# Attention and three binary convolutions on one core: the weighted sums copied out of PSUM by two engines, and the 3x3's products moved ahead in the TensorE order

## The chip, the cores and the metric

The kernel runs on one core of one Trainium2 chip. The metric is the device time of one execution in microseconds (us), lower is better.

## The reference

Two layers act on x of shape (8, 64, 64, 64), eight images of 64 channels and 4096 pixels. The first is an attention over the pixels of each image with an extra "unary" term, the second the sum of a 1x1, a 3x3 and a 5x5 convolution of signs with signs, scaled by a gate per channel. Cut to what matters:

```python
q, k, v = wq@x + bq, wk@x + bk, wv@x + bv          # 64 x 4096 per image
q, k = q - q.mean(pixels), k - k.mean(pixels)
out = softmax(q^T k / 8) applied to v               # 4096 x 4096 per image
out = out + v @ softmax(q_mean . k)                 # the unary term
x = x + out
# second layer
s = sum over k in (1, 3, 5) of bn_k(conv_k(sign(x + move_k), sf_k * sign(w_k - mean)))
gate = sigmoid(grouped 16x16 linear of mean(s))
return s * gate + x
```

## The kernel before

Two images make a **pair**: 128 partitions are two times 64 channels. There are four pairs, done one after the other. A pair's 4096 queries are cut into eight **blocks** of 512 (`QB`), so there are 32 blocks, numbered g = 0 to 31 in `attend`.

Within a block, `for j in range(NK)` goes over 32 groups of 128 keys. Each step issues the scores of step j (`scores`, L474: matmuls into a two-bank PSUM tile `ps` of the pool `ps_s`, which has two such tiles), then exp on ScalarE (L485), then the weighted sums of step j-1 (`weighted`, L493: matmuls that add into `acc`), and on VectorE the sum of the exponentials (`summed`, L506 and L508). So when j = 0 of block g runs, the last weighted sums of block g-1 are still to come; after them the block's own extra work is issued, in an order written out by hand in `plan`: `put(i, f)` issues f after step i.

[...]`ps_s` has two tiles of two banks, `ps_a` one tile of two banks (tag `acc`), `ps_m` two tiles of one bank (tag `m`). The two banks of `acc` hold, per query block, the weighted sums of the two halves of each key group. A tile of a pool takes over the banks of an older one, and waits until that one has been read.

At step 0 of block g the order is:

1. `weighted_out` of block g-1 (L515): ScalarE copies the two banks of `acc` to SBUF, as one tile `o` of 128 x 1024.
2. `send` and `gather` (L522, L530): SP's queue takes the sums of the exponentials through DRAM to spread them over partitions.
3. `mix_rows`: TensorE makes the queries of block g+1 (`split_queries`, L460, into two `m` tiles `pq`, read out by VectorE at L467 and by ScalarE at L468), and from g = 3 on the convolutions of block g-3. At the end of the mix come the read-outs.
4. In some blocks small extra matmuls: `unary_end` (g = 1, 8, 16, 24), `mean_scores` (g = 4, 12, 20), `mean_rows_out` (g = 2).

In `mix_rows` two sequences run side by side on the two row halves of TensorE's array, the rows h = 0 and h = 1, for both images at once, so one step is four small matmuls. Each product has a length in units (0.5 for a product of the 3x3 or 5x5, 1.0 for the 1x1, 2.0 for the queries), and the steps are sorted by it. The second sequence holds products of the 5x5, named A, B and D (25). The first holds the 10 products S of the 5x5, the 1x1, and the 12 of the 3x3, named A, B, S and D too, three of each. The 5x5's S, A and B are in a two-bank tile of `ps_s`, its D and the 1x1 in `m` tiles; the latter take over the banks of the two `pq`, the 1x1 that of L467. **The 3x3 is in a two-bank tile of `ps_a`, the banks of `acc`.** It therefore comes between the weighted sums of block g-1 and those of block g.

The results leave PSUM by `begin_rows` (ScalarE, L729: the 1x1), `hold_rows` (ScalarE, L734: the 3x3, after its last product) and `add_rows` (VectorE, L744 twice and L750: the 5x5's A, B and S). At step 12 of the block, `added` (VectorE, L582) adds the two halves of `o`, and `finish` (L586, L587) divides and adds the residual.

In the last block `weighted_out` is called after the loop with two parts of 320 and 192 columns, since the rest of the work hangs on it. The first queries of all are made in a two-bank tile of `ps_s` and read by VectorE (L442) and ScalarE (L443); the second ones, read by the same two lines, in two `m` tiles. A fallback at the end, for inputs whose exponentials leave the range, does not run here.

The semaphores between engines are set by the tile framework that the kernel is written in. The order of the instructions on each engine is that of the source (`tc.manual_schedule()`).

Of the kernel before, what the change touches and what calls it, by code (L numbers as in the profile page):

```python
# [22 lines left out]
ALU = mybir.AluOpType  # L23
# [3 lines left out]
P = 128  # L27
# [4 lines left out]
QB = 512  # L32
# [12 lines left out]
def conv_seq_kernel(ctx, tc, x, wq, wk, wv, vecs, w1, w3, w5, wtap, gw, out):  # L45
    nc = tc.nc
# [9 lines left out]
    fp = ctx.enter_context(tc.tile_pool(name="fp", bufs=1))  # L56
# [6 lines left out]
    def m_tile(name):  # L63
        return ps_m.tile([P, QB], F32, tag="m", name=name)
# [180 lines left out]
    def n_products(k, name):  # L245
        return k if k == 3 or name == "D" else 2 * k
# [10 lines left out]
    class Pair:  # L257
# [252 lines left out]
        def weighted_out(self, qb, parts=(slice(0, QB),)):  # L510

            acc = self.acc[qb]
            self.acc[qb] = self.tile(fp, "o", qb, (P, 2, QB))
            for c in parts:
                nc.scalar.copy(self.acc[qb][:, :, c], acc[:, :, c])  # L515

# [59 lines left out]
        def added(self, qb, cols=slice(0, QB)):  # L578
            if cols.start == 0:
                self.x2[qb] = self.tile(bp, "x2", qb)  # L580
            acc = self.acc[qb]
            nc.vector.tensor_tensor(self.x2[qb][:, cols], acc[:, 0, cols], acc[:, 1, cols], ALU.add)  # L582

        def finish(self, qb, cols=slice(0, QB)):
            x2 = self.x2[qb][:, cols]
# [295 lines left out]
    def mix_rows(q, c):  # L881


        seqs = [[], []]
        if q is not None:
            for h in range(2):
                seqs[h].append((("q",), 0, 2.0))
        if c is not None:
            p, (r0, _, y) = c
            qb = r0 // ROWS  # L890

            def products(k, name):
                return [((k, name), i, 0.5) for i in range(n_products(k, name))]

            S = products(5, "S")
            three = [t for name in "ABSD" for t in products(3, name)]
            seqs[0] += S[:8] + [((1,), 0, 1.0)] + three + S[8:]
            seqs[1] += products(5, "A") + products(5, "B") + products(5, "D")
        order = []
        for h, seq in enumerate(seqs):  # L900
            at = 0.0
            for t in seq:
                order += [(at, h, b, t) for b in (h, 1 - h)]
                at += t[2]
        order.sort(key=lambda o: o[0:2])
        if q is not None:
            q[0].query_tiles(q[1])
        z, left = {}, {}
        for o in order:
            left[o[3][0]] = left.get(o[3][0], 0) + 1  # L910
        half = [slice(0, QB // 2), slice(QB // 2, QB)]
        for _, h, b, (n, i, _) in order:
            if n == ("q",):
                q[0].split_queries(q[1], b, h)
            else:
                if n not in z:
                    name = f"{p.name}_{qb}_{n[0]}"
                    if n == (1,):
                        z[n] = m_tile(f"z{name}")
                    elif n == (5, "D"):  # L920
                        z[n] = m_tile(f"z{name}d")[:, half[0]]
                    elif n[0] == 3:
                        z3 = ps_a.tile([P, 2, QB], F32, tag="acc", name=f"z{name}")
                        for j, m in enumerate("ABSD"):
                            z[3, m] = z3[:, j // 2, half[j % 2]]
                    else:
                        t = score_banks(f"z{name}")
                        z[5, "S"], z[5, "A"], z[5, "B"] = t[0][:, half[0]], t[1][:, half[0]], t[1][:, half[1]]
                if n == (1,):
                    p.conv_tap((r0, ROWS, y), [[z[n]]], b, 0, 0, 0, True, True)  # L930
                else:
                    p.row_product(z[n], b, *n, i, r0)
            left[n] -= 1
            if left[n] == 0 and n == ("q",):
                q[0].split_queries_out(q[1])
            elif left[n] == 0 and n == (1,):
                p.begin_rows(qb, z[n])
            elif left[n] == 0 and n == (3, "D"):
                p.hold_rows(qb, z3)
        if c is not None:  # L940
            p.add_rows(qb, z[5, "A"], z[5, "B"], z[5, "S"])
            p.z5d = z[5, "D"]
# [21 lines left out]
    def attend(pairs):  # L964
# [9 lines left out]
        def plan(g):  # L974
# [17 lines left out]
            def both():  # L992
                q = block(g + 1) if g + 1 < n_blocks else None
                if g == 0:
                    mix(q, None)
                else:
                    mix_rows(q, rows(g - 3) if g >= 3 else None)
# [291 lines left out]
```

## Time and profile before

| | |
|---|---|
| median of 3 runs | 1933.31 us (1933.23 to 1934.18) |
| profiled execution | 1934.02 us, of which the span from the first to the last instruction is 1931.8 us |
| granted TensorE clock | 0.998 |
| TensorE busy | 1914.2 us, 99% of the span |
| VectorE busy | 1594.1 us, 83% |
| ScalarE busy | 1274.0 us, 66% |
| scores, L474 | 8192 matmuls, 590 ns each |
| weighted sums, L493 | 8192 matmuls, 590 ns each |
| L485 exp, ScalarE | 1024 of 1025 ns |
| L508 sums of exp, VectorE | 960 of 1220 ns |
| L515 copy of `acc`, ScalarE | 31 of 128x1024 at 1006 ns, and two shorter at the end |
| L467 and L468 queries out | 30 of 484 ns and 30 of 490 ns |
| L734 `hold_rows` | 29 of 1114 ns |

Matmuls overlap, so the ends of single ones are modelled and the busy share of TensorE says that it is hardly ever without work, not that it runs at its peak. What matters is the distance between the starts of successive groups: eight matmuls, 0.86 us, for one step's scores or weighted sums. "PEld" is TensorE's weight load. An engine's idle time is put down to what ended it.

### The profile page before, as it was taken

How to read it: one execution, taken by the hardware profiler on the slowest of the kernel's cores; microseconds unless marked ns; L12 is line 12 of the kernel's file. 1: busy time of each engine (PE TensorE's matmuls, PEld its weight loads, DVE VectorE, ACT ScalarE, POOL GpSimd, SP SyncE). 2: the span in 40 equal slices, each digit the busy share in tenths (PEclk: the TensorE clock that was granted, in tenths of full speed). 3: DMA queues.
4: the chain of work that ended last, by engine and by line, in shares of the span. 5: the costliest groups of instructions: out<-in, count | busy, mean ns of one | idle time of the engine just before them, and what ended most of it. 6: DMA issues, size and time to landing. Idle time of an engine off the chain costs nothing.

```text
span 1931.8 us, 48355 instructions
## 1 busy us (share of the span) xinstructions
PE 1914.2 (99%) x20848; PEld 754.9 (39%) x20848; DVE 1594.1 (83%) x2066; ACT 1274.0 (66%) x1523; POOL 5.9 (0%) x26
## 2 busy tenths in 40 slices
PE   9999999999999999999999999999999999999997
PEld 4333343343333333343433333433443333333334
DVE  6878888889887888888888888898887888877876
ACT  5667766666666766666666676666666666666663
POOL 0000000000000000000000000000000000000000
PEclk9999999999999999999999999999999999999999
DMA  3021110110112110101101211011011011111111
GB/s 101 31 70 29 28 40 32 40 35 16 40 35 80 56 51 27 41 32 40 35 16 40 84 53 57 28 29 40 32 40 35 16 56 50 49 39 37 25 35 46
DMA packets 58998, 80.58 MB, mean 42 GB/s; under 512 B 15628, under 2 KB 40600, under 8 KB 58648
## 3 DMA queue, kind: packets, MB, share of 16 engines
q1 hardware_dynamic: 58024, 76.22, 12.9%
q8 instruction: 165, 2.70, 0.6%
q10 hardware_dynamic: 720, 1.18, 0.2%
q14 instruction: 57, 0.47, 0.1%
q0 software_dynamic: 32, 0.01, 0.0%
HBM read 39.27 MB, written 24.77 MB: 33 GB/s over the span
## 4 chain that ended last, share of the span: by engine, by line
PE 97%; DVE 1%; ACT 1%; DMA 0%; issue 0%; SPq 0%; DVEq 0%
PE ps L474 46%; PE acc L493 45%; PE z L703 4%; PE pv L313 1%; PE pq L460 1%; PE z L785 1%; ACT e L485 0%; DMA x<-in_x 0%; DVE es L508 0%; PE warm L155 0%; DVE r L576 0%; PE z_5d L703 0%; DMA out<-sb 0%; ACT o L515 0%; ACT rc_ck L418 0%
## 5 line engine op out<-in xcount | busy, mean ns | idle before, releaser
L485 ACT ACTIVATE e<-ps 128x1024 f32<-128x1024 f32 x1024 | 1049.7, 1025 | 597.8 <-PE ps L474 576.8
L508 DVE TENSOR_TENSOR es<-es,e 128x1024 f32<-128x1024 f32 x960 | 1171.2, 1220 | 187.6 <-ACT e L485 158.2
L474 PE MATMUL ps<-q,x 64*64 64x512 f32 x8192 | 1069.5, 590 | 0.9 <-DVE kb L165 0.9
L493 PE MATMUL acc<-e,v 64*64 64x512 f32 x8192 | 1065.2, 590 | 0.6 <-ACT e L485 0.3
L493 PEld LDWEIGHTS acc<-e,v 64*64 64x64 f32 x8192 | 307.6, 131 | 577.8 <-ACT e L485 305.9
L474 PEld LDWEIGHTS ps<-q,x 64*64 64x64 f32 x8192 | 312.2, 133 | 528.9 <-issue 278.0
L703 PE MATMUL z<-e,wt 64*64 64x256 bf16 x754 | 69.3, 270 | 0.1
L703 PE MATMUL z<-ec,wt 64*64 64x256 bf16 x754 | 69.4, 270 | 0.0
L744 DVE SCALAR_TENSOR_TENSOR sb<-z,scale,sb 128x256 f32<-128x256 f32 x29 | 14.0, 483 | 65.4 <-PE z L703 62.2
L703 PEld LDWEIGHTS <-wt 64*64 64x64 bf16 x1508 | 65.0, 105 | 0.4 <-issue 0.4
L703 PE MATMUL z<-ec,wc 64*64 64x256 bf16 x464 | 60.5, 270 | 0.0
L506 DVE TENSOR_TENSOR es<-e,e 128x1024 f32<-128x1024 f32 x32 | 39.2, 1225 | 24.5 <-ACT e L485 24.5
L703 PEld LDWEIGHTS <-wc 64*64 64x64 bf16 x1218 | 55.6, 106 | 4.8 <-issue 0.6
L619 ACT ACTIVATE s<-x,vec 128x512 bf16<-128x512 f32 (+2 forms) x66 | 46.1, 702 | 5.2 <-DVE x L587 5.2
L757 DVE TENSOR_TENSOR sb<-sb,es_z 128x256 f32<-128x256 f32 x116 | 43.9, 420 | 1.0
L703 PE MATMUL z<-e,wc 64*64 64x256 bf16 x319 | 44.4, 270 | 0.0
L734 ACT ACTIVATE es_z<-z,frac 128x1024 f32<-128x1024 f32 x29 | 32.3, 1114 | 16.3 <-PE z L703 16.3
L515 ACT COPY o<-acc 128x1024 f32<-128x1024 f32 (+2 forms) x33 | 32.3, 981 | 1.2 <-PE acc L493 1.2
L467 DVE TENSOR_SCALAR q<-pq,mx 128x256 f32<-128x256 f32 x30 | 14.5, 484 | 20.8 <-PE pq L460 20.8
L313 PEld LDWEIGHTS pv<-wx,x 64*64 64x64 f32 x1024 | 21.6, 134 | 17.8 <-issue 9.2
L703 PE MATMUL z<-s,wc 64*64 64x256 bf16 x145 | 25.4, 270 | 0.0
L587 DVE SCALAR_TENSOR_TENSOR x<-x,ou,x 128x512 f32<-128x512 f32 (+2 forms) x33 | 24.3, 735 | 1.2
(156 smaller groups left out, 743.6 us busy)
## 6 DMA issues: line engine op xcount, KB each, us to landing
es<-es SPq DMA_DIRECT2D x31, 512.0 KB
e_parts<-es SPq DMA_DIRECT2D x124, 128.0 KB
r<-rc SPq DMA_DIRECT2D x62, 128.0 KB
x<-in_x SPq DMA_DIRECT2D x15, 512.0 KB
out<-sb SPq DMA_DIRECT2D x28, 256.0 KB
ec<-e SPq DMA_DIRECT2D x29, 153.0 KB
xc<-in_x SPq DMA_DIRECT2D x60, 64.0 KB
ec<-e SPq DMA_DIRECT2D x29, 132.0 KB
```

The lines of the kernel that those rows point to most:

```text
L313: nc.tensor.matmul(pv[img[h], b, i * w : (i + 1) * w], self.x[img[b], bass.ds((4 * g + i) * P + h * H, H)], self.wx[img[b], :], start=True ...
L474: nc.tensor.matmul(ps[img[h], b, :], self.x[img[b], bass.ds(j * P + h * H, H)], self.q[qb][img[b], :], start=True, stop=neg is None,)
L485: nc.scalar.activation(e, ps, AF.Exp, scale=1.0 / 8.0)
L493: nc.tensor.matmul(self.acc[qb][img[b], h, :], self.v[img[h], j, img[b]], e[img[h], b, :], start=(j == 0), stop=(j == NK - 1),)
L506: nc.vector.tensor_tensor(self.es[qb], self.first, e, ALU.add)
L508: nc.vector.tensor_tensor(self.es[qb], self.es[qb], e, ALU.add)
L515: nc.scalar.copy(self.acc[qb][:, :, c], acc[:, :, c])
L587: nc.vector.scalar_tensor_tensor(x2, x2, self.ou, self.x[:, bass.ts(qb, QB)][:, cols], ALU.add, ALU.add)
L619: nc.scalar.activation(sy[n][0][:, rows, pad : pad + HH], self.x2[qb][:, r0 * HH : r1 * HH].rearrange("p (h w) -> p h w", w=HH), AF.Sign, ...
L703: nc.tensor.matmul(z[img[b], :].rearrange("p (h w) -> p h w", w=HH), taps[img[h], c * C : c * C + C], src[:, first : first + 3 * step + 1 ...
L734: nc.scalar.activation(z, two, AF.Identity, scale=frac[3][:, 0:1])
L757: nc.vector.tensor_tensor(out, out, self.z3[i], ALU.subtract if (i, t) == (3, 1) else ALU.add)
```

## The change

Three edits. `weighted_out` copies the two banks of `acc` with two instructions in place of one: ScalarE copies the first bank to a tile `o0`, VectorE the second to a tile `o1`. `added` adds the two tiles. In `mix_rows`, the first sequence was eight products S, the 1x1, the twelve of the 3x3, two S; it becomes five S, six of the 3x3 (A and B), the 1x1, six of the 3x3 (S and D), five S. The number of matmuls is the same.

```diff
         def weighted_out(self, qb, parts=(slice(0, QB),)):

             acc = self.acc[qb]
-            self.acc[qb] = self.tile(fp, "o", qb, (P, 2, QB))
+            self.acc[qb] = [self.tile(fp, f"o{h}", qb) for h in range(2)]
             for c in parts:
-                nc.scalar.copy(self.acc[qb][:, :, c], acc[:, :, c])
+                nc.scalar.copy(self.acc[qb][0][:, c], acc[:, 0, c])
+                nc.vector.tensor_copy(self.acc[qb][1][:, c], acc[:, 1, c])
...
             acc = self.acc[qb]
-            nc.vector.tensor_tensor(self.x2[qb][:, cols], acc[:, 0, cols], acc[:, 1, cols], ALU.add)
+            nc.vector.tensor_tensor(self.x2[qb][:, cols], acc[0][:, cols], acc[1][:, cols], ALU.add)
...
             S = products(5, "S")
             three = [t for name in "ABSD" for t in products(3, name)]
-            seqs[0] += S[:8] + [((1,), 0, 1.0)] + three + S[8:]
+            seqs[0] += S[:5] + three[:6] + [((1,), 0, 1.0)] + three[6:] + S[5:]
             seqs[1] += products(5, "A") + products(5, "B") + products(5, "D")
```

## The prediction

> **What bounds the kernel now.** I read the page's engine table first, then the waits, then the timeline of one block boundary, because the change touches nothing else.
>
> ```profile
> PE 1914.2 (99%) x20848; PEld 754.9 (39%) x20848; DVE 1594.1 (83%) x2066; ACT 1274.0 (66%) x1523; POOL 5.9 (0%) x26
> ACT e L485 <- PE ps L474: 576.8, 865, 3.1
> DVE sb L744 <- PE z L703: 62.2, 28, 2.2
> PEld acc L493 <- ACT es_z L734: 22.2, 29, 0.9
> DVE q L467 <- PE pq L460: 20.8, 29, 0.7
> ```
>
> The first line is the engine table, the others are from the waits (who waited for whom: us in total, times, longest). TensorE is the bound: ScalarE and VectorE wait for it, not it for them. What it loses near this change, it loses where a block of 512 queries ends, 31 times. There, 29 times, its weight load waits for ScalarE's L734 (`hold_rows`), and 29 times VectorE stands idle 0.72 us (20.8/29) before it copies the queries out.
>
> The timeline at the boundary near 602 us (start, us, engine, line, out<-in, idle before):
>
> ```profile
> 601.61 1.04 PE L493 MATMUL acc<-e,v 64*64 64x512 f32 x8
> 602.77 1.01 ACT L515 COPY o<-acc 128x1024 f32<-128x1024 f32 x1
> 603.13 0.48 DVE L467 TENSOR_SCALAR q<-pq,mx 128x256 f32<-128x256 f32 x1 [0.72 <-PE pq L460]
> 603.78 0.38 PE L785 MATMUL z<-y,wt 64*64 64x512 bf16 x2
> 605.54 1.11 ACT L734 ACTIVATE es_z<-z,frac 128x1024 f32<-128x1024 f32 x1 [0.56 <-PE z L703]
> 605.68 1.03 PE L474 MATMUL ps<-q,x 64*64 64x512 f32 x6
> 606.71 1.09 PE L493 MATMUL acc<-e,v 64*64 64x512 f32 x8
> 607.62 0.61 PE L474 MATMUL ps<-q,x 64*64 64x512 f32 x4
> ```
>
> Query products start at 602.46, the products of the convolutions at 602.89, one step of four small matmuls every 0.11 us, 25 steps. The 1x1 starts at step 8, the 3x3 at step 10 (604.00). The 3x3 uses the `acc` banks, so it must follow the copy L515, which ends at 603.78: 0.2 us to spare, no wait. At the other end `hold_rows` ends at 606.65 and only then do the next weighted sums start, at 606.71. The scores before them (605.68) take 0.86 us in the steady loop, so 606.54 was possible; with the exposed weight load the next scores start at 607.62 instead of 607.41. **The bubble is 0.205 us.** Start times at all 28 boundaries from 189 to 1781 us show it 22 times; in the other six (near 250, 488, 722, 961, 1194, 1433 us), where `unary_end` or `mean_scores` puts extra matmuls before the scores, there is none. The most that can be gained is thus about 22 x 0.205 = 4.5 us, 0.23%.
>
> [...] VectorE COPY out of PSUM takes 290 ns for 128 columns and 356 for 192, 1.03 ns a column. [...]
>
> **Do the two copies run side by side?** The kernel leaves semaphores to its tile framework, so I looked for two engines that read one two-bank PSUM tile. There is one place: the first queries, whose `pq` is a tile of the scores pool, bank 0 read by VectorE (L442), bank 1 by ScalarE (L443). A second time the same two lines read two separate tiles. The timeline of the two engines there:
>
> ```profile
> 12.18 0.74 DVE L442 TENSOR_SCALAR q<-pq,mx 64x512 f32<-64x512 f32 x1
> 13.02 0.68 ACT L443 ACTIVATE q<-pq,nmx 64x512 f32<-64x512 f32 x1 [1.91 <-DVE kb L165]
> 14.89 1.02 ACT L485 ACTIVATE e<-ps 128x1024 f32<-128x1024 f32 x1 [1.19 <-PE ps L474]
> 15.94 0.68 ACT L443 ACTIVATE q<-pq,nmx 64x512 f32<-64x512 f32 x1
> L443 ACTq EVENT_SEMAPHORE  x1: 17/17/17, 12.9 to 12.9; - x1
> ```
>
> The first L443 was idle 1.91 us. Its data were ready (`pq` before 7.7 us, `nmx` at 12.20), yet its EVENT_SEMAPHORE (last line, from the answer for that source line) passed only at 12.9 and it started at 13.02; L442 had ended at 12.92. The second L443 has no such semaphore, though it too writes `q` beside L442. What differs is the shared PSUM tile. L744 points the same way: it reads products A in one bank, all done by 605.3, and starts at 605.84, after the last S product in the other bank. So waits go by tile, not bank, reads against reads included. `acc` is such a tile. **I take it that the VectorE copy waits for the ScalarE copy**, and that the 3x3, which takes over the tile, waits for both.
>
> **The change, part by part** (boundary near 602 us).
>
> 1. ScalarE copies 512 columns instead of 1024: 586 ns (L321, the same shape from PSUM) instead of 1006, 602.77 to 603.36. ScalarE is not the bound; its saved 0.42 us is covered by TensorE.
> 2. VectorE copies 512: no row has it. From the slope, 290 + 384 x 1.03 = 686 ns (upper end 743, L442's time). It starts 0.03 us after ScalarE's: 603.39 to 604.08. Queued behind it is L467: 604.0 to 604.5, 0.87 us late. Who waits: the 1x1 takes L467's bank, but comes later (604.80), so nothing; the new `q` is wanted a block later.
> 3. The 3x3 moves from step 10 to step 5, 603.45 undisturbed. It now needs the VectorE copy: 604.08 + 0.04 to pass the semaphore + about 0.03 of exposed weight load = 604.15. **Stall 0.70 us** (0.62 if the wait hides behind a loaded weight and the copy is short, 0.80 with the longest copy). [...] everything behind stalls: 1x1, S, A, B, D, the scores. No DMA moves: SP issues its `send` and `gather` as before, ahead of these products.
> 4. The 3x3 ends three steps earlier relative to the rest, so `hold_rows` starts 0.33 us earlier in relative terms. Its own predecessor on ScalarE, the 1x1's L729, comes 0.33 us later and just clears. Then it ends about 0.2 us before the weighted sums want the banks: the bubble of 0.205 goes. What is late next is the release of the S, A, B banks (L750 ends 607.17 + 0.70), which the second scores meet with a few hundredths to spare.
> 5. L582 adds two SBUF tiles instead of halves of one: same 684 ns.
>
> Sum: 22 boundaries x (0.70 - 0.205) = 10.9. Six without a bubble x 0.70 = 4.2. The one at 1840 us (no query products, copy already late by 0.26): 3x3 released at 1841.07, 20 steps follow, scores 0.88 later less the bubble: 0.7. The first two have no convolutions, but `unary_end` (76.45) and `mean_rows_out` (133.18) use L467's bank and wait for it already: L467 later by 0.65 and 0.86: 1.5. Last block: two parts, each copied by both engines, alternating (0.43, 0.49, 0.32, 0.36 us by the slopes): L582 moves from 1905.39 to 1906.25, the reciprocals L576 from 1905.89 to 1906.66: 0.8. **Total +18.1 us.** The profiled execution took 1934.02 (span 1931.8), 0.71 above the median of 1933.31; on the median the forecast is 1951.4.
>
> **Rivals.** A measurement of this kernel can tell about 0.2%, 3.9 us, from no change.
> - *Side by side, wait by tile.* VectorE starts when TensorE's last sum is done, 602.70 to 603.39, inside its 0.72 us of idle time. The 3x3's weights can load at 603.43: stall at most 0.05. Gain 22 x 0.16 - 6 x 0.05 = 3.2, less 0.8 for L467 in the first two blocks: 1930.9. [...] Against: the semaphore at 12.9 us. It decides if the VectorE copy starts before ScalarE's ends; with its extras it wins while the stall is under 0.13 us, that is with the copy over by about 603.5.
> - *One after the other, but each half of the 3x3 waits for its own bank.* A and B need ScalarE's half (603.41), S and D come at 604.32, after VectorE's. No stall: gain 4.5, less 1.5 and 0.8: 1931.1. Against: L744.
> - *Side by side without any stall* and little lost in the first two blocks: 22 x 0.205 = 4.5, 1929 or a little less, just past what can be told. That needs waits by bank throughout.
>
> **How the numbers follow.** One after the other 0.85 (slower); side by side by tile or each half by its bank 0.10 (the same); no stall at all 0.05 (faster). Within the first, the stall of 0.62 to 0.80 gives 15.8 to 20.9; without first blocks and tail 2.3 less, with unseen waits of 0.1 at each boundary about 3 more: 1946 to 1957, and I reach one lower.
>
> **What would show it.** Right: a VectorE COPY `o1` starting 0.03 us after ScalarE's `o0` ends, 686 ns long; TensorE's first 3x3 product waiting 0.6 to 0.8 us for it, 29 times, some 20 us in all; the wait of L493 for L734 gone; L467 near 1.6 us after the queries begin. Wrong: both copies starting within 0.1 us of each other, or no wait of L703 for VectorE.

## The result

The changed kernel takes **1949.58 us** (median of 4, 1948.93 to 1950.35) against 1933.74 for the kernel before in the same comparison (1933.23 to 1934.77): the ratio is 1.0081, 95% interval 1.0064 to 1.0099. It is 15.8 us slower; 18.1 were forecast, and the measured time lies within the forecast range. The profiled execution has a span of 1947.1 us, 15.3 more than before, at the same granted clock of 0.998.

The page of the changed kernel, its span, its engines and two of its groups:

```profile
span 1947.1 us, 48392 instructions
PE 1915.5 (98%) x20848; PEld 895.2 (46%) x20848; DVE 1612.2 (83%) x2099; ACT 1257.2 (65%) x1523; POOL 5.9 (0%) x26
L704 PE MATMUL z<-e,wt 64*64 64x256 bf16 x754 | 74.8, 271 | 14.9 <-DVE o L516 14.9
L516 DVE COPY o<-acc 128x512 f32<-128x512 f32 (+2 forms) x33 | 22.3, 676 | 29.8 <-ACT o L515 29.8
```

VectorE has 18 us more to do and ScalarE 17 less, as the edit says, and neither matters. What matters stands at the end of the last two lines (idle time before the group, and what ended how much of it): the VectorE copy is held 29.8 us by the ScalarE copy, and TensorE's products by the VectorE copy. The waits of the changed kernel:

```profile
DVE o L516 <- ACT o L515: 29.8, 32, 1.0
PE z L704 <- DVE o L516: 14.9, 29, 0.9
PEld acc L493 <- ACT es_z L735: 13.6, 26, 0.6
```

And its timeline at the same boundary as before (line numbers after L515 are one higher):

```profile
606.32 0.58 ACT L515 COPY o<-acc 128x512 f32<-128x512 f32 x1
606.78 0.49 ACT L468 ACTIVATE q<-pq,nmx 128x256 f32<-128x256 f32 x1
606.93 0.69 DVE L516 COPY o<-acc 128x512 f32<-128x512 f32 x1 [0.97 <-ACT o L515]
607.54 0.48 DVE L467 TENSOR_SCALAR q<-pq,mx 128x256 f32<-128x256 f32 x1
607.67 0.27 PE L704 MATMUL z<-e,wt 64*64 64x256 bf16 x1 [0.50 <-DVE o L516]
609.47 1.10 ACT L735 ACTIVATE es_z<-z,frac 128x1024 f32<-128x1024 f32 x1
609.78 0.61 PE L474 MATMUL ps<-q,x 64*64 64x512 f32 x2
610.64 1.17 PE L493 MATMUL acc<-e,v 64*64 64x512 f32 x8
```

The copies are not side by side. ScalarE's ends at 606.90, VectorE's begins at 606.93 and ends at 607.62, TensorE's first 3x3 product follows at 607.67. VectorE's read-out of the new queries (L467) now comes 0.76 us after ScalarE's (L468), which does not wait for the second copy. The last two lines are the first scores after the mix and the weighted sums behind them.

### The profile page after: what moved, and what is told of

Read it like the earlier page. It is cut to its first block, busy times and chain, and to the rows that moved or that the text cites. A ratio compares the mean times of both kernels' runs of the same rounds, so it can differ in the third digit from the quotient of the medians.

```text
span 1947.1 us, 48392 instructions
## 1 busy us (share of the span) xinstructions
PE 1915.5 (98%) x20848; PEld 895.2 (46%) x20848; DVE 1612.2 (83%) x2099; ACT 1257.2 (65%) x1523; POOL 5.9 (0%) x26
## 4 chain that ended last, share of the span: by engine, by line
PE 94%; ACT 3%; DVE 2%; issue 0%; DMA 0%; DVEq 0%
PE ps L474 45%; PE acc L493 43%; PE z L704 3%; ACT e L485 2%; DVE o L516 1%; ACT o L515 1%; PE pv L313 1%; PE z L786 1%; PE warm L155 0%; DVE es L508 0%; DVE r L577 0%; PE z_5d L704 0%; DMA out<-sb 0%; ACT rc_ck L418 0%; PE po L363 0%
## 5 line engine op out<-in xcount | busy, mean ns | idle before, releaser
L474 PE MATMUL ps<-q,x 64*64 64x512 f32 x8192 | 1115.1, 590 | 0.9 <-DVE kb L165 0.9
L493 PE MATMUL acc<-e,v 64*64 64x512 f32 x8192 | 1112.4, 589 | 0.6 <-ACT e L485 0.3
L474 PEld LDWEIGHTS ps<-q,x 64*64 64x64 f32 x8192 | 398.6, 133 | 442.9 <-issue 223.4
L493 PEld LDWEIGHTS acc<-e,v 64*64 64x64 f32 x8192 | 355.2, 131 | 525.0 <-ACT e L485 307.8
L704 PE MATMUL z<-e,wt 64*64 64x256 bf16 x754 | 74.8, 271 | 14.9 <-DVE o L516 14.9
L704 PE MATMUL z<-ec,wt 64*64 64x256 bf16 x754 | 74.7, 272 | 0.0
L730 ACT ACTIVATE sb<-z,shift,scale 128x512 f32<-128x512 f32 x29 | 22.6, 778 | 44.4 <-PE z L786 44.4
L516 DVE COPY o<-acc 128x512 f32<-128x512 f32 (+2 forms) x33 | 22.3, 676 | 29.8 <-ACT o L515 29.8
L321 ACT COPY v<-pv 128x512 f32<-128x512 f32 x32 | 18.8, 586 | 9.3 <-PE pv L313 9.2
```

Of the source, the lines that this page charges most:

```text
L474: nc.tensor.matmul(ps[img[h], b, :], self.x[img[b], bass.ds(j * P + h * H, H)], self.q[qb][img[b], :], start=True, stop=neg is None,)
L493: nc.tensor.matmul(self.acc[qb][img[b], h, :], self.v[img[h], j, img[b]], e[img[h], b, :], start=(j == 0), stop=(j == NK - 1),)
L516: nc.vector.tensor_copy(self.acc[qb][1][:, c], acc[:, 1, c])
L704: nc.tensor.matmul(z[img[b], :].rearrange("p (h w) -> p h w", w=HH), taps[img[h], c * C : c * C + C], src[:, first : first + 3 * step + 1 ...
```

## The experiments

**Theory:** the framework's semaphores keep order by PSUM tile. Two engines that only read different banks of one tile wait for each other, and whoever takes the tile over waits for both. **Rivals:** the moved order itself costs the time; or two engines cannot read PSUM at once, whatever the semaphores say; or the second engine is what matters, not the tile.

Diffs are against the changed kernel, except in "Which part of the two-tile kernel does it", where they are against the two-tile kernel with both engines; they show what matters. The kernels were timed against the kernel before (1933.78 us; for the change itself, 1933.74). "Regular" is the mean delay per block over the 22 boundaries that had a bubble, "other six" over those without one, taken from the starts of the scores and weighted sums in the two traces (a block here runs from the last weighted sums of one block to the last of the next).

| kernel | median, us | ratio (95%) | regular, us | other six, us |
|---|---|---|---|---|
| the change | 1949.58 | 1.0081 (1.0064 to 1.0099) | +0.45 | +0.74 |
| new order only | 1940.10 | 1.0032 (1.0019 to 1.0044) | +0.16 | +0.44 |
| two copies only | 1938.96 | 1.0027 (1.0018 to 1.0037) | +0.15 | +0.14 |
| VectorE's copy first | 1949.47 | 1.0078 (1.0065 to 1.0092) | +0.40 | +0.69 |
| two tiles, both engines, new order | 1930.20 | 0.9980 (0.9971 to 0.9988) | -0.25 | +0.04 |
| two tiles, both engines, old order | 1932.45 | 0.9994 (0.9985 to 1.0002) | -0.14 | +0.14 |
| two tiles, ScalarE alone, new order | 1929.31 | 0.9975 (0.9966 to 0.9985) | -0.25 | +0.05 |

### The new order without the second copy

```diff
-            self.acc[qb] = [self.tile(fp, f"o{h}", qb) for h in range(2)]
+            self.acc[qb] = self.tile(fp, "o", qb, (P, 2, QB))
             for c in parts:
-                nc.scalar.copy(self.acc[qb][0][:, c], acc[:, 0, c])
-                nc.vector.tensor_copy(self.acc[qb][1][:, c], acc[:, 1, c])
+                nc.scalar.copy(self.acc[qb][:, :, c], acc[:, :, c])
...
```

> The new order of the products with the single ScalarE copy of before. Theory (the 3x3 waits for every reader of the two banks): the copy of 1006 ns ends 1.32 us after the queries begin, the 3x3 could start at 0.99, so it stalls 0.3 to 0.4 us; less the bubble of 0.205 us where there is one, that is 22 x 0.13 + 6 x 0.34 and a little at the last block: about 5 us slower than before, 1938.5 (1936 to 1941). If instead the moved order itself costs what the change cost (rival: the copies are innocent), it is 1949 as after the change.

1940.10. The wait is there with the name changed, in the waits of this kernel:

```profile
PE z L703 <- ACT o L515: 6.2, 29, 0.6
```

So the order costs 6.3 us by itself, and not the 15.8 of the rival: it asks for the banks before the single copy has let go of them.

### The two copies without the new order

```diff
-            seqs[0] += S[:5] + three[:6] + [((1,), 0, 1.0)] + three[6:] + S[5:]
+            seqs[0] += S[:8] + [((1,), 0, 1.0)] + three + S[8:]
```

> The two copies in the old order of the products. Theory: VectorE starts when ScalarE ends and is over 1.61 us after the queries begin; the 3x3 of the old order is due at 1.54, so it stalls 0.1 to 0.15 us 29 times and the bubble of 0.205 us stays: about 4 us slower than before, 1937.5 (1935 to 1940). If the copies ran side by side it would be 1933.5, as before; if the 1x1 takes the bank that VectorE's late read-out of the queries frees, 0.8 us more at each boundary, 1957.

1938.96, within the range. The scores after the mix start 0.13 us later (0.13 to 0.15) at all 28 boundaries, bubble or not. Its timeline has the same chain; the two engines' copies:

```profile
604.78 0.58 ACT L515 COPY o<-acc 128x512 f32<-128x512 f32 x1
605.40 0.69 DVE L516 COPY o<-acc 128x512 f32<-128x512 f32 x1 [0.96 <-ACT o L515]
```

The two edits share one reserve. Before, the 3x3 came about 0.17 us after the copy let go. The pair of copies ends 0.30 us later than the single one (1.61 instead of 1.31 after the queries begin), the new order asks 0.55 us earlier: alone they stall by 0.13 and 0.38, together by 0.30 + 0.55 - 0.17 = 0.68. By these three amounts the scores start later at most regular boundaries of the three traces. That is why 6.3 and 5.2 us add up to less than 15.8.

### VectorE's copy first

```diff
-                nc.scalar.copy(self.acc[qb][0][:, c], acc[:, 0, c])
                 nc.vector.tensor_copy(self.acc[qb][1][:, c], acc[:, 1, c])
+                nc.scalar.copy(self.acc[qb][0][:, c], acc[:, 0, c])
```

> The changed kernel with the two copies issued in the other order, VectorE's first. Theory: ScalarE now waits for VectorE. VectorE starts 0.24 us after the queries begin (ScalarE had to finish an exp first, 0.31), the pair ends at 1.55 instead of 1.61: about 2 us faster than the changed kernel, 1947.5 (1946 to 1949), ScalarE's copy starting 0.03 us after VectorE's ends. If only VectorE were made to wait: both at once, 1930.

The order of the waits turned with the order of issue, as expected: ScalarE's copy now starts at 609.66, when VectorE's, begun at 608.93, is over. Two lines of its timeline:

```profile
608.93 0.69 DVE L515 COPY o<-acc 128x512 f32<-128x512 f32 x1 [0.29 <-PE acc L493]
609.66 0.59 ACT L516 COPY o<-acc 128x512 f32<-128x512 f32 x1 [0.56 <-DVE o L515]
```

The time was a miss: 1949.47, no gain that can be told. In the profiled execution, which took 1950.76, the boundaries gain 0.05 us each, 28 x 0.05 = 1.4 us, but block 1 takes 2.3 us longer than in the changed kernel. Of that 0.6 is `unary_end` waiting for VectorE's L467, and 1.7 is a TensorE at half clock (0.51 for 3.4 us), of which more below. Without the half clock 0.8 us would be gained, too little to be seen in five executions that lie 2 us apart.

### Two tiles of one bank

```diff
-                self.acc[qb] = ps_a.tile([P, 2, QB], F32, tag="acc", ...)
+                self.acc[qb] = [ps_a.tile([P, QB], F32, tag=f"acc{h}", ...) for h in range(2)]
...
-                        z3 = ps_a.tile([P, 2, QB], F32, tag="acc", name=f"z{name}")
+                        z3 = [ps_a.tile([P, QB], F32, tag=f"acc{h}", name=f"z{name}{h}") for h in range(2)]
...
+            elif left[n] == 0 and n == (3, "B"):
+                p.hold_rows(qb, z3, 0)
             elif left[n] == 0 and n == (3, "D"):
-                p.hold_rows(qb, z3)
+                p.hold_rows(qb, z3, 1)
```

> The changed kernel, with the two banks of the weighted sums as two PSUM tiles of one bank each in place of one tile of two, and so the 3x3's, whose read-out by ScalarE is cut in two instructions (A and B as soon as they are done, S and D at the end). Theory (the wait goes by tile, reads against reads included): both copies now start within 0.1 us of each other, the 3x3 is not stalled, the bubble goes: 3 to 4 us faster than before, 1929.8 (1928 to 1932). Rival (the engines themselves can't read PSUM at once, or VectorE's copy is late for its own reasons): VectorE still starts after ScalarE ends, 1946 to 1950.

1930.20: 3.6 us faster than before and 19 faster than the change, with the same copies on the same engines and the same order of products. Part of its edit is that the 3x3 is read out in two instructions, one tile each, instead of one. That is not what brings the 19 us: in both kernels the first weighted sums start 0.86 us behind the scores, and what is gone is the stall ahead of them. At the regular boundaries the scores start 0.65 to 0.73 us sooner than in the changed kernel, within 0.12 us of where they stood before the change. The timeline of both engines at this boundary:

```profile
602.58 0.58 ACT L515 COPY o<-acc 128x512 f32<-128x512 f32 x1
604.11 0.69 ACT L737 ACTIVATE es_z<-z,frac 128x512 f32<-128x512 f32 x1 [0.57 <-PE z L704]
605.36 0.69 ACT L737 ACTIVATE es_z<-z,frac 128x512 f32<-128x512 f32 x1
602.54 0.69 DVE L516 COPY o<-acc 128x512 f32<-128x512 f32 x1 [0.32 <-PE acc L493]
```

VectorE starts at 602.54, before ScalarE at 602.58, and both take as long as one after the other: 0.69 and 0.58 us. Here two engines read two PSUM tiles of one bank each at once, and neither copy took longer for it; the second rival is out. What was missing was a program that lets them.

### The clue of the prediction, tried

```diff
-        first.query_tiles(0, score_banks)
+        first.pq = [score_banks("pq_0_0")[0], acc_banks("pq_0_0b")[1]]
```

> The changed kernel, with the first queries (L442, L443) in banks of two different PSUM tiles, one of the scores pool and one of the weighted sums' pool, in place of the two banks of one tile. Theory: ScalarE's L443 no longer waits for VectorE's L442 and starts as soon as nmx is written, within 0.15 us of L442's start instead of 0.84 after it. Rival (L443 waited for something else, the write into q or nmx): 0.8 us after it, as before. The whole time stays within 1.5 us of the changed kernel's.

ScalarE's first L443 now starts 0.13 us after VectorE's L442, and is released by `nmx`. From the timeline of the two engines:

```profile
12.02 0.74 DVE L442 TENSOR_SCALAR q<-pq,mx 64x512 f32<-64x512 f32 x1
12.15 0.68 ACT L443 ACTIVATE q<-pq_0b,nmx 64x512 f32<-64x512 f32 x1 [1.19 <-DVE nmx L296]
```

In the changed kernel it is 0.84:

```profile
11.87 0.74 DVE L442 TENSOR_SCALAR q<-pq,mx 64x512 f32<-64x512 f32 x1
12.71 0.68 ACT L443 ACTIVATE q<-pq,nmx 64x512 f32<-64x512 f32 x1 [1.91 <-DVE kb L165]
```

The one place of the trace before that told the forecast's sign was read rightly: the shared tile held L443, not `q` and not `nmx`. One execution took 1948.95.

### Which part of the two-tile kernel does it

ScalarE alone, copying one tile after the other:

```diff
-                nc.vector.tensor_copy(self.acc[qb][1][:, c], acc[1][:, c])
+                nc.scalar.copy(self.acc[qb][1][:, c], acc[1][:, c])
```

> As the kernel with two tiles of one bank (new order, the 3x3's read-out in two), but ScalarE copies both banks, one after the other, and VectorE none. Theory: a product waits for its own bank alone; ScalarE's first copy is over 0.9 us after the queries begin, before the 3x3's A and B at 0.99, the second at 1.4, before S and D at 1.87: no stall, and VectorE's read-out of the queries is no longer late in the first blocks and in those with mean_scores. 5 us faster than before, 1928.5 (1927 to 1930), and 1 to 2 faster than with the two engines. Rival (it was the second engine that gained): a stall of 0.4 us as in the order-only kernel, 1938.

**1929.31 us, the fastest of all**, 4.5 us faster than before. The copies at a boundary, and its waits:

```profile
601.40 0.58 ACT L515 COPY o<-acc 128x512 f32<-128x512 f32 x1
601.87 0.60 ACT L516 COPY o<-acc 128x512 f32<-128x512 f32 x1
602.94 0.69 ACT L737 ACTIVATE es_z<-z,frac 128x512 f32<-128x512 f32 x1
```

```profile
PEld acc L493 <- ACT es_z L737: 4.7, 23, 0.2
```

No product of the 3x3 waits for a copy: A and B need the first, S and D come late enough for the second. The third rival is out too, for in the new order the second engine brought nothing. The medians of this kernel and of the one with both engines differ by 0.9 us, within their intervals; the traces put 0.8 of it into blocks 1 and 2, where VectorE's copy makes L467 late.

The old order with two tiles and both engines:

```diff
-            seqs[0] += S[:5] + three[:6] + [((1,), 0, 1.0)] + three[6:] + S[5:]
+            seqs[0] += S[:8] + [((1,), 0, 1.0)] + three + S[8:]
```

> Two tiles of one bank, both engines copying, but the old order of the products. Theory: the bubble at the end goes here too, since S and D alone are left to read out after the last product of the 3x3 (0.69 us instead of 1.11) and the first weighted sums find their bank free; what the new order adds is little. VectorE's read-out of the queries is 0.05 to 0.1 us late for the 1x1 at step 8, if that takes its bank. 1930.5 (1928.5 to 1932.5). Rival (the order is what takes the bubble away): 1933.5, with L493 still waiting for the 3x3's read-out.

1932.45, at the upper end of what was expected; whether it is faster than before can't be told. In its waits the bubble is gone all the same:

```profile
PEld acc L493 <- ACT es_z L737: 4.4, 24, 0.3
```

It was 22.2 us in the kernel before. The starts say so more surely: near 602 us the first weighted sums come 0.86 us behind the first scores (608.45 and 607.59), where before it was 1.15 (606.71 and 605.56), and it is 0.86 at all 22 boundaries that had the bubble. So in the old order the split tile and the split read-out together remove the bubble (they were not tried apart); in the new order the order alone does, as the change and the kernel with the new order only show, also with 0.86. The new order is worth 2.2 us on top (1932.45 - 1930.20). The two traces put 0.11 us of it, one step, at each of the 28 boundaries, less some 0.4 us that block 31 gives back. It fits the 1x1 at step 8 waiting for VectorE's late L467, which is read from the starts alone:

```profile
605.29 0.48 DVE L467 TENSOR_SCALAR q<-pq,mx 128x256 f32<-128x256 f32 x1
605.82 0.40 PE L788 MATMUL z<-y,wt 64*64 64x512 bf16 x2
```

The copies by ScalarE alone in the old order were not tried.

## Why the prediction was right, by its steps

- **One copy after the other.** Right: VectorE starts 0.03 us after ScalarE ends (0.03 forecast) and takes 692 ns (686 from the slope of two smaller copies).
- **The stall of 0.70 us.** Right to a few hundredths. The scores after the mix start 0.68 us later at sixteen regular boundaries, where ScalarE's copy starts 0.31 us after the queries, as before. They start 0.77 later at the six others of these 22, the one shown among them, where the copy starts at 0.40, and 0.69 to 0.80 later at the six without a bubble. The 14.9 us in the waits, where some 20 were forecast, count only the time in which no earlier product was still running (0.51 us at each).
- **The bubble goes.** Right: 0.68 - 0.205 = 0.475 against a measured mean of 0.45. My sign for it was wrong: the weight load of L493 is still listed as waiting for `hold_rows`, 13.6 us, yet the weighted sums start at 610.64, 0.86 us behind the first scores of 609.78, which is the distance of the steady loop. In this run these waits under running matmuls cost nothing.
- **The sum.** Forecast and measured, in us of the span: 22 regular boundaries 10.9 and 10.0; the other six 4.2 and 4.4; block 31 0.7 and 0.7; the last block's tail 0.8 and 0.4; blocks 1 and 2 1.5 and 0.1; the start, where nothing changes, 0 and -0.3. Together 18.1 and 15.3.
- **The term that was mis-sized is that of blocks 1 and 2.** The step said: `unary_end` and `mean_rows_out` "use L467's bank". They did before. In the changed kernel they use L468's, and L468 is not delayed. The wait before the change, the wait after it, and block 1 after it:

```profile
PEld po L363 <- DVE q L467: 1.3, 1, 1.3
```

```profile
PEld po L363 <- ACT q L468: 1.3, 1, 1.3
75.63 0.47 ACT L468 ACTIVATE q<-pq,nmx 128x256 f32<-128x256 f32 x1
76.16 0.38 PE L363 MATMUL po<-ones,vu 128*128 128x1 f32 x2 [0.83 <-ACT q L468]
76.25 0.48 DVE L467 TENSOR_SCALAR q<-pq,mx 128x256 f32<-128x256 f32 x1
```

`unary_end` (L363) starts before L467 does, so it cannot have waited for it. Nor does the 1x1 take L467's bank where both copies stand in the old order: there it starts at 605.79 and L467 at 606.00. I had kept the banks fixed while changing the copies, and with them the banks moved. How the framework picks a bank is not shown. In the kernels in which VectorE copies without waiting (VectorE first, two tiles with both engines) the name is L467 again and block 1 is 0.6 us later, as the step had it, though in the one with two tiles L468 is over first (76.61 against 77.19).
- **The tail** moved by 0.77 us up to the last copy out of PSUM, as worked out; about 0.4 came back between that copy and the end of the span, where only transfers and the end of the program are left. That was not looked into.

## What to carry to other kernels

Before giving two engines two halves of a buffer, find one place in the trace where two engines already share such a buffer and see whether the second one starts with the first or after it (here L443 began 0.84 us after L442 with one tile and 0.13 us with two). If waits are kept by tile, allocate what is to be used apart as tiles of its own: that was worth 19 us here against the changed kernel, 3.6 to 4.5 against the kernel before, and the second engine nothing (1930.20 us with it, 1929.31 without). An earlier start of a consumer and a later end of its producer drew on the same reserve here: they are added up and the slack is subtracted once (0.55 + 0.30 - 0.17 = 0.68 us).

## What the runs showed that I had not expected

In the traces of two kernels, VectorE's copy first and two tiles in the old order, TensorE stood idle for 1.40 and 1.41 us in block 1, waiting for L467. It resumed, and 1.8 us later in the one and 1.2 us later in the other it ran at half clock for about 3.4 us. In a third, two tiles with both engines in the new order, it was idle for 1.41 us too and kept its clock. The first product after the pause in each of the three, in this order:

```profile
77.41 0.38 PE L363 MATMUL po<-ones,vu 128*128 128x1 f32 x2 [1.40 <-DVE q L467]
76.90 0.38 PE L363 MATMUL po<-ones,vu 128*128 128x1 f32 x2 [1.41 <-DVE q L467]
77.25 0.38 PE L363 MATMUL po<-ones,vu 128*128 128x1 f32 x2 [1.41 <-DVE q L467]
```

The windows behind it (us from the start, the length, then busy time and number of each engine's instructions, then the granted clock, DMA share and GB/s): three of VectorE's copy first, two of two tiles in the old order, one of two tiles in the new order.

```profile
77.40:79.30 1.90, 1.89 (x16) 1.03 (x20) 0.39 (x2) 1.46 (x7) 0.00 (x0) 0.98 0.57 229
79.30:82.70 3.40, 3.40 (x21) 1.06 (x17) 1.23 (x1) 1.36 (x2) 0.00 (x0) 0.51 0.53 166
82.70:85.00 2.30, 2.30 (x28) 0.92 (x24) 1.73 (x2) 1.25 (x2) 0.00 (x0) 1.00 0.14 40
```

```profile
77.40:79.30 1.90, 1.90 (x13) 0.64 (x17) 0.39 (x2) 1.09 (x5) 0.00 (x0) 0.70 0.31 123
79.30:81.70 2.40, 2.40 (x16) 0.79 (x12) 1.22 (x1) 0.60 (x1) 0.00 (x0) 0.53 0.64 203
```

```profile
79.30:82.70 3.40, 3.40 (x37) 1.21 (x32) 2.15 (x2) 2.02 (x3) 0.00 (x0) 1.00 0.55 172
```

A clock of 0.51 for 3.4 us costs 1.7 us, which is what block 1 lost besides the wait itself. In these two traces the clock fell to 0.51 and 0.53 after a gap of 1.40 and 1.41 us. That the gap is the cause is not shown, and the third trace, with a clock of 1.00 after 1.41 us, shows that it is not enough.

The program alone does not seem to decide it either. Each trace is of one execution, and the mean clocks of the others differ. Of thirteen executions of two tiles in the old order, the five longest (1933.44 to 1934.35 us), the profiled one among them, had a mean clock of 0.996 and the other eight 0.997 or 0.998. Of five of VectorE's copy first, the two longest (1950.76 and 1950.86 us), the profiled one among them, had 0.996 and the other three 0.997. By an estimate, 3.4 us at half clock lower the mean over 1930 us by 0.0009. So probably only some executions of one program have this stretch; without traces of the others that is not shown.
